# A first-pass timetable: the channel mix placed over all of its 4.5 slots, the input normalisation behind the key's high half

## The chip, the core and the metric

The kernel runs on one core of a Trainium2 chip. The metric is the device time of one execution, in microseconds (us). The core's engines are TensorE (PE, matmuls; PEld its weight loads), VectorE (DVE), ScalarE (ACT), GpSimd (POOL), and SyncE (SP), whose queue issues all of this kernel's DMAs. Each engine works through its own instructions in one order and stands where an instruction has to wait.

## The reference

The input `x` has 8 sequences of 1024 tokens and 512 channels. It is normalised, and two layers work on the result `xn`; their outputs are added to `x`.

```python
xn  = layernorm(x)
out = x + attn(xn) + ffn(xn)

# attn: Performer attention (16 heads of 32, 128 random features), then an MLP
pq, pk = phi(q), phi(k)         # exp(proj - |u|^2/2 - max(proj)) / sqrt(128) + 1e-6
kv, z  = sum_s pk v, sum_s pk   # over all 1024 tokens of a sequence
h      = (pq kv) / (pq z) @ wo
x1     = layernorm(xn + h) * g1 + b1
attn   = layernorm(x1 + gelu(x1 @ w1 + b1) @ w2 + b2) * g2 + b2

# ffn: channel mix with the token before
xr, xk = mu_r*xn + (1-mu_r)*xn_prev, mu_k*xn + (1-mu_k)*xn_prev
ffn    = sigmoid(xr @ Wr) * (relu(xk @ Wk)**2 @ Wv)
```

## The kernel before

Every large matmul is done in float16 with a high and a low half of each operand: `mm3` adds up high x high, high x low and low x high, 12 matmuls of 128x128 by 512 over four slices of 128 channels. So each operand is first made in float32, copied to float16 on ACT (the high half), and subtracted from its copy on DVE or POOL (the low half).

**Two passes.** In the first the tokens go in units of 128 (64 units, `i` or `b, u`) through normalisation, value, key, key features and the sums `kv` and `z`; beside it the channel mix layer (`ffn_k`, `ffn_r`, `ffn_o`) goes through blocks of 512 tokens (16 blocks, `bk`). The second pass does queries, attention output and the MLP. Between them the pools of the key are closed and those of the query opened.

**The timetable.** All work is written as generators that are entered with `at(tau, f, ...)`, where `tau` is a due time in slots of 15.4 us (`us(t)` is t / 15.4 slots). A heap takes the step that is due next and emits its instructions; `yield d` puts the rest of the generator back, due `d` later. So due times do not time anything on the chip: they fix the order of instructions on each engine. In the first pass the order on PE, DVE, ACT, POOL and SP is pinned to the order of emission (`Pinned`, `chained`). At slot 72.55 (`TK`) all but PE are let go of, until slot 81.55, and the scheduler of the framework orders them.

**A slot of the first pass**, with due times in us within the slot: the weights' product for the key (`proj_a`) on PE at 2.56, its high half `u` on ACT at 5.21, low half `u` on DVE at 6.41, its store `ud` and transposed copy `uT` on SP at 7.61, the three loads of `skk` (`proj_l`) on SP at 10.6; the key's norm (`norm`): POOL at 12.6, which reads `uT`, ACT 4.0 and DVE 10.0 later. The key features (`KB`), two parts a slot: PE at 9.0 and 14.56, then a maximum `mxk` and the bias `bik` on DVE, eight exps and a high half `ekh` on ACT, a low half `ekl` on DVE. The value (`V`): PE at 9.45, ACT at 12.15, DVE low half `v` at 13.65. `KC`, `KD`, `KE` add up and divide the sums (`kvp`, `kvz`, bank `kac`). Statistics of the input (`Ls`, `Lr`) are on DVE. `Ln` normalises a unit: ACT Identity in place on `xt`, ACT high half, POOL low half, then on SP a transposing DMA into `xb` and the store `xn_d`. One unit of `Ln` is due each slot, and `V` reads it three slots later.

**PSUM.** The results of `V` (`psv`), `proj_a` (`psu`), `ffn_k` (`psk`), `ffn_r` (`psr`) and `ffn_o` (`psf`) take turns in three banks (`mmt`), so a matmul group may start only when the result of three groups earlier has been read, by DVE's low half in the case of `V` and `proj_a`. `KB` has two buffers of its own, `pj`.

**The channel mix.** `ffn_k`, `ffn_r` and `ffn_o` have 12 groups a block, in spots at 0, 5.12 and 12 us of a slot, every ninth spot left out; a block thus takes 4.5 slots. `tau` of a block is the due time of its first `ffn_k`. What that reads is made by `mix(bk, p)`, called for p = 0 and 1, two channel slices (`w`) each: POOL adds the halves of `xb` to `xs` (513 columns) and takes the difference `df` of neighbouring tokens; DVE makes `xm` for k and for r from them; then for k and for r ACT writes the high half of `mx` and DVE the low half (1024 columns, two slices). `xs` and `df` have one buffer each, `xm` two. The first `ffn_k` takes the slices of p = 0 first and those of p = 1 behind them.

Of the kernel before, what the change touches and what calls it, by code (L numbers as in the profile page):

```python
# [11 lines left out]
F16 = mybir.dt.float16  # L12
# [11 lines left out]
BLK = 512  # L24
# [36 lines left out]
def block_kernel(ctx, tc, x, wq, wk, wv, wo, om3, ln1_g, ln1_b, w1, b1, w2, b2,  # L61
# [100 lines left out]
    def st(shape, dt, name, bufs=2, tag=None):  # L162
        tag = tag or name
        pool = pools["k"] if tag in KPOOL else pools["c"] if tag in CPOOL else pools["q"] if tag in QPOOL else sp
        return pool.tile(shape, dt, name=name, tag=tag, bufs=bufs)
# [25 lines left out]
    def us(t):  # L191
        return t / 15.4
# [14 lines left out]
    def warp(j, t):  # L207
        while t >= 27.68:
            j, t = j + 1, t - 27.68
        if j not in warps:  # L210
            r, tab = 0.0, []
            for a, d in slot_pe(j):
                d = max(d, 0.02)
                tab.append((a, r, d))
                r += d
            warps[j] = tab, r
        tab, ln = warps[j]
        a, r, d = [e for e in tab if e[0] <= t + 1e-6][-1]
        nx = min([e[0] for e in tab if e[0] > t + 1e-6], default=27.68)
        return TM + j + (r + (t - a) / (nx - a) * d) / ln  # L220
# [316 lines left out]
    mixd = {}  # L537
    kact = {}
    rr = {}

    def mix(bk, p):
        b, blk = divmod(bk, 2)
        hh, ll = xblk[b, blk]
        if p == 0:
            mixd[bk] = {nm: st([128, 2, 4, BLK], F16, "mx4", 4) for nm in "kr"}
        xm = {nm: st([128, 2, BLK], F32, "xm", 2) for nm in "kr"}
        o = XO - 1
        for w in range(2):
            c = p * 2 + w
            xs = st([128, BLK + 1], F32, "xs", 1)  # L550
            gps.tensor_tensor(xs, hh[:, c, o:o + BLK + 1], ll[:, c, o:o + BLK + 1], ALU.add)
            yield us(1.5)
            df = st([128, BLK], F32, "df", 1)
            gps.tensor_tensor(df, xs[:, 1:BLK + 1], xs[:, 0:BLK], ALU.subtract)
            yield us(4.0)
            for nm, mu in (("k", muk), ("r", mur)):
                dve.scalar_tensor_tensor(
                    xm[nm][:, w], df, mu[:, c:c + 1], xs[:, 0:BLK], ALU.mult, ALU.add
                )
                yield us(1.2)  # L560
        yield us(1.2)
        cs = slice(p * 2, p * 2 + 2)
        for nm in "kr":
            m = mixd[bk][nm]
            act.copy(m[:, 0, cs, :], xm[nm])
            yield us(3.2)
            dve.tensor_tensor(m[:, 1, cs, :], xm[nm], m[:, 0, cs, :], ALU.subtract)
            yield us(0.4)

    def ffn_k(bk, d):  # L570
        if d == 0:
# [282 lines left out]
    def at(tau, f, *a):  # L854
        ev.append((tau, len(ev), f, a))
# [17 lines left out]
    for i in range(NU):  # L873
        b, u = divmod(i, 8)
        at(i - 5 + us(0.5) if i > 5 else -9, Lx, i)
        at(i - 4 + us(4.9) if i > 3 else -7, Ls, i)
        if u % 4 == 0:
            at(i - 1 + us(7.3) if i else -6, Lr, i // 4)
        at(i + us(3.3) if i > 3 else -5 + 0.1 * i, Ln, b, u)
        if u % 4 == 3:  # L880
            at(i + 1.5, xstore, b, u // 4)
        at(i + 3 + us(9.45), V, b, u)
        at(i + 4 + us(2.56), proj_a, "k", b, u)
        at(i + 4 + us(10.6), proj_l, "k", b, u)
        at(i + 4 + us(12.6), norm, "k", b, u)
        at(i + 5 + us(9.0), KB, b, u, 0)
        at(i + 5 + us(14.56), KB, b, u, 1)
        at(i + 7 + us(7.7), KC, b, u)
        if u >= 4:
            at(i + 8 + us(2.53), KD, b, u - 4)  # L890
            at(i + 9 + us(7.65 if b < NB - 1 else 0.0), KE, b, u - 4)
# [4 lines left out]
    for bk in range(NBK):  # L896
        for k, (nm, a) in enumerate(GR):
            tau = spots[bk * 12 + k]
            if k == 0:
                for p in range(2):  # L900
                    at(tau - 2.7 + 1.25 * p, mix, bk, p)
            at(tau, {"k": ffn_k, "r": ffn_r, "o": ffn_o}[nm], bk, a)
    for k in range(32):
        at(12.3 + 1.5 * k, split_mlp, k)
# [4 lines left out]
    for i in range(NU):  # L909
        b, u = divmod(i, 8)  # L910
# [35 lines left out]
    for n in range(NBK):  # L946
        for t in range(4):
            if n == 0:
                tau = TQ + 6.5 + 0.3 * (t // 2) + 0.01 * (t % 2)
# [23 lines left out]
        for fc in range(16):  # L973
            s = j + fc // 4
            k = fc % 4
            tau = warp(s, (0.0, 2.56, 10.84, 16.56)[k])
# [34 lines left out]
    while todo:  # L1011
        tau, k, f, a = heapq.heappop(todo)
# [59 lines left out]
```

## Time and profile before

| | us |
|---|---|
| three runs, median (lowest to highest) | 3019.23 (3014.38 to 3019.41) |
| the profiled execution | 3021.76 |
| its span, first to last instruction | 3020.0 |
| TensorE busy in it | 2798.8 (93%) |
| VectorE, ScalarE, GpSimd busy | 2306.8, 1756.3, 990.9 |
| mean granted TensorE clock | 0.972 |

All times in the prediction's sums are from the one profiled execution. A busy time is the union of an engine's instructions in a stretch; an idle stretch is put down to what was released last before the instruction that ended it. A line such as `PE psk L137 <- DVE mx L185: 15.6, 6, 5.9` says that TensorE, ahead of matmuls that write `psk`, waited 15.6 us in total for a DVE instruction that writes `mx`, in 6 places, the longest 5.9. L137 and L185 are lines of helpers through which every instruction goes, so rows are told apart by tiles.

### The profile page before, as it was taken

What the parts mean: (1) busy time and instruction counts of PE and PEld (TensorE: products, weight loads), DVE (VectorE), ACT (ScalarE), POOL (GpSimd) and SP (SyncE); (2) the same over time, 40 slices, a digit from 0 to 9 for tenths busy, and PEclk for the clock granted to TensorE, in tenths of its full rate; (3) what the DMA queues carried; (4) which work ended last, traced back from release to release, by engine and by line L of the source; (5) the groups of instructions that cost most, each with busy time, mean ns of one, the idle gap of its engine ahead of it and who ended that gap; (6) DMA issues with size and microseconds to landing.
All of it is one profiled execution on the core that took longest, in us unless ns stands there. A gap on an engine that the chain in (4) does not pass through costs nothing. (4 is left out here: it accounts for less than half of the span.)

```text
span 3020.0 us, 52198 instructions
## 1 busy us (share of the span) xinstructions
PE 2798.8 (93%) x18784; PEld 1392.0 (46%) x18784; DVE 2306.8 (76%) x4456; ACT 1756.3 (58%) x3828; POOL 990.9 (33%) x860
## 2 busy tenths in 40 slices
PE   3999999999999884999999999999999999999996
PEld 1454444444445442444444444444444444444442
DVE  5898888888888756567777777777787787787654
ACT  4888888888888654454554554554554544554210
POOL 3444444554444323123222232232232232232111
PEclk7999999999999997999999999999999999999998
DMA  6567666666665288877777777777687677776432
GB/s 192 142 168 180 172 165 170 171 178 172 171 161 139 70 192 182 189 161 176 177 164 175 179 167 174 168 175 177 167 179 172 166 182 172 161 187 155 122 101 84
DMA packets 839348, 494.82 MB, mean 164 GB/s; under 512 B 632016, under 2 KB 718128, under 8 KB 837040
## 3 DMA queue, kind: packets, MB, share of 16 engines
q1 hardware_dynamic: 839088, 491.49, 66.6%
q8 instruction: 147, 2.41, 0.3%
q14 instruction: 113, 0.93, 0.1%
HBM read 226.95 MB, written 113.38 MB: 113 GB/s over the span
## 5 line engine op out<-in xcount | busy, mean ns | idle before, releaser
L137 PE MATMUL psw<-x1b,w1s 128*128 128x512 f16 x3072 | 695.3, 380 | 0.0
L137 PE MATMUL acc<-w2h,gg 128*128 128x512 f16 x2048 | 650.6, 380 | 2.0 <-DVE gg L185 1.9
L137 PEld LDWEIGHTS <-w1s 128*128 128x128 f16 x3072 | 295.9, 98 | 343.8 <-issue 2.5
L137 PEld LDWEIGHTS <-gg 128*128 128x128 f16 x3072 | 293.6, 98 | 329.0 <-issue 4.4
L185 ACT ACTIVATE g<-psw,b1t 128x512 f32<-128x512 f32 x256 | 172.7, 686 | 394.5 <-PE psw L137 351.4
L137 PE MATMUL acc<-w2l,gg 128*128 128x512 f16 x1024 | 389.1, 380 | 0.0
L185 ACT ACTIVATE e<-pj,biq 128x128 f32<-128x128 f32 x1024 | 291.9, 370 | 153.8 <-DVE biq L185 121.5
L185 ACT ACTIVATE e<-pj,bik 128x128 f32<-128x128 f32 x1024 | 280.9, 393 | 106.5 <-DVE bik L185 106.3
L185 POOL TENSOR_TENSOR eq<-e,eq 128x512 f16<-128x512 f32 x128 | 167.3, 1307 | 415.9 <-ACT eq L185 271.3
L185 POOL TENSOR_TENSOR u<-ot,u 128x512 f16<-128x512 f32 x64 | 84.1, 1314 | 662.4 <-ACT u L185 638.0
L185 DVE TENSOR_REDUCE mxq<-pj 128x4 f32<-128x512 f32 x256 | 175.2, 686 | 118.6 <-PE pj L137 117.6
L185 POOL TENSOR_TENSOR e<-u 128x512 f32<-128x512 f16 x128 | 174.3, 1361 | 181.0 <-DMA u<-u 160.6
L185 ACT ACTIVATE u<-psu 128x512 f16<-128x512 f32 x128 | 76.4, 597 | 235.9 <-PE psu L137 233.4
L185 DVE TENSOR_SCALAR gg<-g 128x512 f16<-128x512 f32 x256 | 107.9, 422 | 132.9 <-ACT g L185 132.8
L185 DVE SCALAR_TENSOR_TENSOR gg<-g,gg 128x512 f16<-128x512 f32 x256 | 188.9, 738 | 8.8
L137 PE MATMUL psv<-whv,xb 128*128 128x512 f16 x512 | 166.5, 387 | 20.0 <-DMA xb<-u 20.0
L137 PE MATMUL psu<-xb,whk 128*128 128x512 f16 x512 | 159.3, 394 | 27.6 <-DVE v L185 21.5
L185 ACT ACT_TABLE_LOAD x114 | 146.3, 1283 | 61.0 <-DVE biq L185 53.5
L185 DVE SCALAR_TENSOR_TENSOR ekl<-e,ekh 128x1024 f16<-128x1024 f32 x128 | 180.6, 1411 | 0.2
L137 PE MATMUL psk<-mx,whfk 128*128 128x512 f16 x512 | 157.2, 386 | 18.2 <-DVE mx L185 18.0
L137 PE MATMUL psf<-whfv,kx 128*128 128x512 f16 x512 | 163.4, 381 | 9.9 <-DVE u L185 9.9
L137 PE MATMUL psr<-whfr,mx 128*128 128x512 f16 x512 | 167.6, 390 | 2.2 <-DVE v L185 1.5
(160 smaller groups left out, 5627.1 us busy)
## 6 DMA issues: line engine op xcount, KB each, us to landing
w1s<-w1d SPq DMA_DIRECT2D x256, 256.0 KB, 3.0
ud<-u SPq DMA_DIRECT2D x128, 256.0 KB, 2.7
skk<-ud SPq DMA_DIRECT2D x192, 128.0 KB, 2.7
skq<-ud SPq DMA_DIRECT2D x192, 128.0 KB, 3.2
xt<-in_x SPq DMA_DIRECT2D x64, 256.0 KB, 3.5
xnd<-xt SPq DMA_DIRECT2D x64, 256.0 KB, 2.4
xtd<-xb SPq DMA_DIRECT2D x16, 1024.0 KB, 5.8
ffd<-rsg SPq DMA_DIRECT2D x64, 256.0 KB, 2.4
```

The lines of the kernel that those rows point to most:

```text
L137: return chained("pe", nc.tensor.matmul(*a, **k))
L185: return lambda *a, **k: chained(self.key, f(*a, **k))
```

## The change

The heap, the generators' instructions and their number stay; due times change, and with them the order on ACT, DVE, POOL and SP.

- `mix` gets a third argument `f`. From `df` to the first `xm` it waits 3.0 instead of 4.0 us, between the `xm` steps and behind them 2f instead of 1.2, from a high half to its low half 3.0 instead of 3.2, behind the low half 2f instead of 0.4. A pair of slices takes 15 + 14f us up to the due time of its last low half.
- The two halves of `mix` were due at tau − 2.7 and tau − 1.45 slots and overlapped. Now they follow one another: the first starts at tau − 4.5, but not before 4bk + 3.95 (when the block's last unit has been normalised); the second at tau − 2.3, or half-way from the first to tau − 0.3 where there is less room. `f` is worked out so that each fills its time. It is −0.11 in block 0, 0.07 in block 1, 0.44, 0.62, 0.99 in blocks 2 to 4, and 1.35 and 1.13 for the two halves from block 6 on.
- The buffers of `mx` are taken when the first high half is written, not at the start of `mix`.
- `Ln` is due at 5.6 instead of 3.3 us of its slot: its Identity and high half on ACT come behind the key's high half (5.21), and its two DMAs behind `ud` and `uT`.

```diff
-    def mix(bk, p):
+    def mix(bk, p, f):
         b, blk = divmod(bk, 2)
         hh, ll = xblk[b, blk]
-        if p == 0:
-            mixd[bk] = {nm: st([128, 2, 4, BLK], F16, "mx4", 4) for nm in "kr"}
+        mixd.setdefault(bk, {})
...
             gps.tensor_tensor(df, xs[:, 1:BLK + 1], xs[:, 0:BLK], ALU.subtract)
-            yield us(4.0)
+            yield us(3.0)
             for nm, mu in (("k", muk), ("r", mur)):
                 dve.scalar_tensor_tensor(
                     xm[nm][:, w], df, mu[:, c:c + 1], xs[:, 0:BLK], ALU.mult, ALU.add
                 )
-                yield us(1.2)
-        yield us(1.2)
+                yield us(2.0 * f)
+            yield us(2.0 * f)
         cs = slice(p * 2, p * 2 + 2)
         for nm in "kr":
+            if p == 0:
+                mixd[bk][nm] = st([128, 2, 4, BLK], F16, "mx4", 4)
             m = mixd[bk][nm]
             act.copy(m[:, 0, cs, :], xm[nm])
-            yield us(3.2)
+            yield us(3.0)
             dve.tensor_tensor(m[:, 1, cs, :], xm[nm], m[:, 0, cs, :], ALU.subtract)
-            yield us(0.4)
+            yield us(2.0 * f)
...
-        at(i + us(3.3) if i > 3 else -5 + 0.1 * i, Ln, b, u)
+        at(i + us(5.6) if i > 3 else -5 + 0.1 * i, Ln, b, u)
...
             if k == 0:
-                for p in range(2):
-                    at(tau - 2.7 + 1.25 * p, mix, bk, p)
+                m0 = max(4 * bk + 3.95, tau - 4.5)
+                m1 = max((m0 + tau - 0.3) / 2, tau - 2.3)
+                at(m0, mix, bk, 0, ((m1 - m0) * 15.4 - 15.0) / 14.0)
+                at(m1, mix, bk, 1, ((tau - 0.3 - m1) * 15.4 - 15.0) / 14.0)
```

## The prediction

> **What bounds the kernel now.** I read the page's engine shares and slices first, then busy time by stage, then TensorE's waits in the first pass, then VectorE's rows ahead of the longest wait. From the page:
>
> ```profile
> PE 2798.8 (93%) x18784; PEld 1392.0 (46%) x18784; DVE 2306.8 (76%) x4456; ACT 1756.3 (58%) x3828; POOL 990.9 (33%) x860
> ...
> PE   3999999999999884999999999999999999999996
> DVE  5898888888888756567777777777787787787654
> ACT  4888888888888654454554554554554544554210
> ```
>
> TensorE (PE) is the bound nearly everywhere; in the first third VectorE (DVE) and ScalarE (ACT) are nearly as full. By stage (start, first pass, changeover, second pass; columns: busy time and count per engine, then granted clock):
>
> ```profile
> 0.00:110.00 110.00, 61.27 (x343) 28.37 (x344) 68.78 (x132) 66.53 (x131) 43.50 (x49) 0.86 0.60 164
> 110.00:1010.00 900.00, 847.77 (x6252) 439.00 (x6251) 774.27 (x1253) 747.13 (x1717) 423.90 (x406) 0.98 0.64 167
> 1010.00:1240.00 230.00, 164.62 (x1215) 83.27 (x1214) 138.92 (x285) 121.95 (x297) 71.23 (x62) 0.84 0.70 160
> 1240.00:3020.00 1780.00, 1725.17 (x10980) 841.40 (x10977) 1324.87 (x2788) 820.66 (x1687) 452.26 (x344) 0.99 0.69 163
> ```
>
> The edited steps lie in the first pass and its two ends. There TensorE idles 900 − 847.8 = 52 us. The 472 high key matmuls (8 a slot) make 59 slots in those 900 us: 15.25 us each. Who TensorE waits for there (total, times, longest):
>
> ```profile
> PE psk L137 <- DVE mx L185: 15.6, 6, 5.9
> PE psu L137 <- DVE v L185: 12.4, 9, 2.5
> PE psf L137 <- DVE u L185: 9.9, 5, 3.1
> PE pj L137 <- ACT e L185: 7.7, 6, 2.3
> ...
> PE psr L137 <- DVE v L185: 1.5, 1, 1.5
> ```
>
> The first row is the mix itself: `ffn_k` stands until the second pair's low half of `mx` is written. Rows 2, 3 and 5 are PSUM banks that VectorE frees late (the low halves `v` and `u`). The longest wait on VectorE:
>
> ```profile
> 338.84 0.68 DVE L185 SCALAR_TENSOR_TENSOR rsg<-rsg,psf 128x512 f32<-128x512 f32 x1
> 339.44 1.22 DVE L185 TENSOR_REDUCE mxk<-pj 128x8 f32<-128x1024 f32 x1
> ...
> 343.05 1.22 DVE L185 TENSOR_TENSOR mx<-xm,mx 128x1024 f16<-128x1024 f32 x1
> 344.18 0.68 DVE L185 SCALAR_TENSOR_TENSOR v<-psv,v 128x512 f16<-128x512 f32 x1
> ```
>
> VectorE has no gap here; it works through a queue some microseconds behind the timetable, and `psk` starts as `mx` ends (344.3, after 5.94 idle).
>
> **The change, part by part.** No instruction is added or removed; every mix instruction, and the five of `Ln`, change place in an order fixed per engine.
>
> *1. The wait on `mx`.* Before, the second pair starts at tau − 1.45 slots and its k low half falls due 18.2 + 3.2 = 21.4 us later: 0.93 us ahead of `ffn_k`. After, for blocks 6 to 15, it starts at tau − 2.3 with f = 1.13, and is due 9 + 12f + 3 = 25.5 us later: 9.9 us ahead. (Block 0: 7.4, block 2: 8.5, block 4: 9.6.) The longest wait is 5.9, the move 6.5 to 9, so all go: 15.6, and 2.5 of the same kind at the start: **−18**.
>
> *2. The clock behind those waits.* Ten microseconds around the waits at 344 and at 894, and around one of 2.5 us at 202:
>
> ```profile
> 195.00:205.00 10.00, 7.47 (x43) 3.58 (x41) 9.83 (x17) 6.94 (x15) 1.76 (x4) 1.00 0.76 212
> 338.00:348.00 10.00, 4.06 (x12) 1.46 (x11) 9.83 (x17) 4.80 (x12) 1.22 (x2) 0.66 0.72 210
> ...
> 890.00:900.00 10.00, 6.85 (x27) 2.74 (x26) 9.53 (x13) 7.12 (x15) 4.20 (x5) 0.83 0.44 119
> ```
>
> 0.83 over 10 us is 1.7 us of lost clock. Seven 512-column matmuls at 634 instead of 379 ns after the wait make the same 1.8. Three of the `mx` waits (344, 757, 894) have such a stretch: **−5**. The Trainium skill, "TensorE: Matmul & The Clock Gate", section "Why this matters for your kernels", asks only that idle gaps stay under about 3 us; by it the 2.04 us gap at 757 would cost nothing, which the granted clock there (0.83) denies, and this term would be −3.4.
>
> *3. The banks.* Mix work on VectorE is, per block, 8 `xm` at 0.90 and 4 `mx` at 1.27 (means over all): 12.3 us. Before, it falls due between tau − 2.3 and tau + 0.2, 2.5 slots, 4.9 us a slot; after, over 3.9 slots, 3.1. VectorE is busy 774 / 59 = 13.1 a slot, so 13.1 − 12.3 / 4.5 = 10.4 without the mix: 15.3 in a mix slot before, as much as a slot lasts (15.25), and 13.5 after. The bank waits lie where that predicts: at 408, 470, 591, 683, 819, 836 and 954, each in the last two slots ahead of a block's tau. `Ln` behind the key's high half helps the same rows: its two ACT steps (0.83 and 0.62 us) no longer delay `u`, for which VectorE waits 69.3 us in 31 places. Rows: 12.4 + 9.9 + 2.2 = 24.5, and three slow-clock stretches (408, 470, 539), 5: between 0 and −30, and above nothing if VectorE comes to wait more (first rival). The mechanism fits but each wait has other feeders, so half: **−15**.
>
> *4. ACT.* `pj <- e`, 7.7 us with two stretches, 3.4: between 0 and −11. Its exps wait for `bik`, which VectorE computes late in the same slots; I take **−3**. `Ln`'s high half now stands between the exps of `KB`'s second part, ahead of all of which it stood before; no exp has more ahead of it.
>
> *5. What `Ln` passes.* On POOL its subtraction goes from 4.7 to 7.0 us, on SP the transposing DMA and the `xn_d` store from 7.3 to 9.6, behind `ud` and `uT` (7.61), ahead of the three `skk` loads (10.6). So the key's store no longer stands behind 1.24 us of transposing issue, 0.58 of store issue and the POOL step they wait for: its gain is at most the `pj <- skk` row, 3.1; I count none. `V` reads `xb` three slots later, so that reader is safe. The mix reads it at 4bk + 3.95 in blocks 0 to 5, 0.33 slot (5 us) after the due issue, and `xb` lands in 3.1 us (median); a late transfer stops POOL with the key norm behind it. POOL is 47% busy, so **0**; without that cover up to some 3 us in each of five blocks, +15.
>
> *6. Ends of the pass.* In the changeover TensorE waits 9.9 us for `kvz` while blocks 14 and 15 are mixed: between 0 and −10 (and their clock), I take **−3**. The order there is free of the timetable for a while and may shuffle by as much again; the second pass (waits of 31 us in 1780) keeps its steps.
>
> *7. What is late next.* −18 − 5 − 15 − 3 − 3 = −44 over 63 slots takes 0.7 us off a slot of 15.25. VectorE then fills 13.1 / 14.55 = 90% and ACT 747 / 59 / 14.55 = 87% (86% and 83% now), both in strict order: waits on banks and `pj` come back elsewhere. I give back a third, between nothing and all of parts 3 to 6 (21): **+15**.
>
> Sum **−29**. The profiled execution took 3021.8 (span 3020.0), 2.5 over the median, so 3021.8 − 29 − 2.5 = 2990.
>
> **The rivals.**
>
> *VectorE waits for POOL (slower).* Each pair of `xm` steps stands behind `df` on POOL. The lead from `df`'s due time to theirs shrinks from 4.0 to 3.0 us, while `xs` and `df` take 1.38 and 1.30; and in the later odd blocks the first `xs` now falls due 0.2 us behind the key norm's add, which waits for its transposed tile:
>
> ```profile
> POOL e L185 <- DMA u<-u: 92.2, 29, 7.9
> ...
> DVE xm L185 <- POOL df L185: 10.4, 7, 2.2
> ```
>
> Were half of the 64 pairs to wait 2.2 us, VectorE would lose 70 instead of 10. It decides against the change once more than the sure gain, 18 + 5 = 23 us, of new stall reaches TensorE; if half of the 60 does and the other parts give nothing, the sum is +7, if three quarters, +22: 3026 to 3041. For it: the seven such waits now. Against: the first `xs` and `df` of even blocks now stand ahead of the norm's add, and the norm comes earlier with the key; today's VectorE stalls (69 + 18 + 10) leave only 24.5 of bank waits.
>
> The Trainium skill, "SBUF — State Buffer", section "Who interferes with whom", speaks against spreading: a VectorE step with two SBUF inputs and a GpSimd step exclude each other. `xm` shows it (735 ns at best, 1698 at worst); if all 128 met one collision, it would be 128 × (1.70 − 0.90) = 102 us more of VectorE, and a mix slot as full as before.
>
> *Only the `mx` waits go.* VectorE's queue is late for other reasons, and half of 23 comes back at the banks: −12, 3007. For it: `psk` waits are the only ones that name the mix. Against: the places in part 3.
>
> *All waits of VectorE's queue go.* −18 − 5 − 30 − 11 with little given back: −50, 2969. For it: nothing but TensorE would then bound the pass. Against: 90% on two engines in strict order.
>
> *It doesn't spread.* Blocks 0 and 1 get less room than before (0.9 and 1.0 slot a pair; f is −0.11 and 0.07), and a POOL that runs late pushes the early steps back to where they were: within 6 us of 3019.
>
> **How the numbers follow.** Forecast (2975 to 3001) 0.45; only `mx` (3001 to 3013) 0.20; all waits (under 2975) 0.13; no spread 0.06; POOL stalls (over 3025) 0.16. 0.2%, about what a measurement of this kernel tells from no change, is 6 us: faster 0.78, same 0.06, slower 0.16. The range 2960 to 3030 cuts the tails of the third and the first rival.
>
> **What would show it.** Right: no `psk <- mx` row; the bank rows at half or less; first pass shorter by some 25 us at a clock of 0.99; the second pass at 1780. Wrong: `xm <- df` over 50 us with bank waits as before or more; POOL waiting for `xb`; or the time saved by 1010 lost again before 1240.

## The result, and the profile after

The changed kernel takes 3022.9 us (median of 17 runs, 3016.1 to 3025.2) against 3017.6 for the kernel before in the same session: a ratio of 1.0017, 95% interval [1.0009, 1.0024]. It is a little slower, by 5 us; 2990 was forecast, with 2960 to 3030 as the range and 0.78 on faster. The time lies in the range; the sign and nearly everything in the sum are wrong.

The profiled execution has a span of 3022.2 us. Its page and its busy times by stage (columns as before):

```profile
PE 2799.8 (93%) x18784; PEld 1392.2 (46%) x18784; DVE 2346.4 (78%) x4456; ACT 1752.7 (58%) x3828; POOL 990.1 (33%) x860
```

```profile
0.00:110.00 110.00, 64.40 (x345) 29.07 (x346) 69.44 (x130) 65.66 (x130) 43.98 (x49) 0.86 0.59 168
110.00:1010.00 900.00, 841.66 (x6195) 434.41 (x6193) 806.16 (x1249) 738.11 (x1704) 422.58 (x405) 0.98 0.63 164
1010.00:1240.00 230.00, 167.62 (x1262) 86.15 (x1259) 144.04 (x289) 126.28 (x308) 72.26 (x62) 0.84 0.70 164
1240.00:3020.00 1780.00, 1726.17 (x10992) 842.53 (x10990) 1326.77 (x2789) 822.67 (x1689) 451.26 (x344) 0.99 0.68 163
```

VectorE is where something new stands. Between 110 and 1010 it is busy 806 us with 1249 instructions, where it was 774 with 1253. The work is the same; its instructions have become longer. TensorE's waits in that stage:

```profile
PE psu L137 <- DVE v L185: 34.6, 18, 5.3
PE pj L137 <- ACT e L185: 7.8, 5, 1.9
PE psr L137 <- DVE v L185: 3.7, 4, 1.4
PE kac L137 <- DVE kvb L185: 3.0, 3, 1.3
PE psr L137 <- DVE u L185: 3.0, 3, 1.5
PE psf L137 <- DVE u L185: 2.5, 2, 1.3
```

The row `psk <- mx`, 15.6 us, is gone as forecast. In its place `psu <- v` went from 12.4 us in 9 places to 34.6 in 18: banks that VectorE's low half of the value frees late. The longest of these waits ends at 589.5. First VectorE ahead of it, then GpSimd in the same microseconds (start, duration):

```profile
584.49 1.04 DVE L185 TENSOR_TENSOR kvp<-kvp,kvr 128x132 f32<-128x132 f32 x1
585.57 1.16 DVE L185 CAST kvz<-kvp 128x132 f16<-128x132 f32 x1
586.76 1.05 DVE L185 TENSOR_TENSOR kvz<-kvp,kvz 128x132 f16<-128x132 f32 x1
587.73 1.11 DVE L185 SCALAR_TENSOR_TENSOR bik<-mxk,nsqk 128x8 f32<-128x8 f32 x1
588.76 0.68 DVE L185 SCALAR_TENSOR_TENSOR v<-psv,v 128x512 f16<-128x512 f32 x1
```

```profile
583.39 1.99 POOL L185 TENSOR_TENSOR u<-e,u 128x512 f16<-128x512 f32 x1 [3.71 <-ACT e L185]
585.34 1.20 POOL L185 TENSOR_TENSOR xs<-xb 128x513 f32<-128x513 f16 x1
...
586.62 1.04 POOL L185 TENSOR_TENSOR df<-xs 128x512 f32<-128x512 f32 x1
587.62 1.20 POOL L185 TENSOR_TENSOR e<-u 128x512 f32<-128x512 f16 x1
```

The first four VectorE steps are small: where nothing disturbs them they take 0.30, 0.23, 0.30 and 0.15 us, 1.0 together. Here they take 4.4. Each begins beside a GpSimd step and ends within 0.2 us after it. `v`, which reads PSUM, takes its usual 0.68. So 3.4 of TensorE's 5.34 us of waiting fall on four small steps that GpSimd held up one after the other. `xs` and `df` are the mix's (second pair of block 8): their new due places, 10.78 and 12.28 us of a slot, lie beside `KD` (11.13) and `bik` (11.3), and the key norm's sum (`e`) follows at 12.6. Blocks 6, 10, 12 and 14 have the same places.

**A measure for that.** For each form of VectorE instruction I took its tenth percentile as the undisturbed duration and added up what instructions took beyond it, where that was over 0.15 us ("held up" below). Between 110 and 1010 it is 92 us in 153 instructions before and 128 us in 197 after. 175 of the 197 end as if they had begun only when a GpSimd step ended (the two times agree within 0.15 us); the other 22 are `xm`, which end about 0.5 us after a GpSimd step. The step that ends so is the mix's `xs` or `df` for 21.5 us before and 37.9 after, and the low half of `Ln` (`u<-xt,u`) for 5.4 and 15.8. Most of the growth of 36 us lies in the small steps, here rows of before and then of after (mean ns behind the comma):

```profile
L185 DVE SCALAR_TENSOR_TENSOR bik<-mxk,nsqk 128x8 f32<-128x8 f32 x119 | 31.3, 263 | 1.8
...
L185 DVE TENSOR_TENSOR kvp<-kvp,kvr 128x132 f32<-128x132 f32 x28 | 12.5, 448 | 1.0
...
L185 DVE CAST kvz<-kvp 128x132 f16<-128x132 f32 x28 | 11.7, 416 | 1.0
```

```profile
L185 DVE SCALAR_TENSOR_TENSOR bik<-mxk,nsqk 128x8 f32<-128x8 f32 x118 | 41.9, 355 | 1.4
...
L185 DVE TENSOR_TENSOR kvp<-kvp,kvr 128x132 f32<-128x132 f32 x28 | 19.2, 685 | 1.0
L185 DVE CAST kvz<-kvp 128x132 f16<-128x132 f32 x28 | 17.0, 609 | 1.0
```

### The profile page after: what moved, and what is told of

Same layout as the page of the kernel before. It is cut to its first block, busy times and chain, and to the rows that moved or that the text cites. A ratio compares the mean times of both kernels' runs of the same rounds, so it can differ in the third digit from the quotient of the medians.

```text
span 3022.2 us, 52191 instructions
## 1 busy us (share of the span) xinstructions
PE 2799.8 (93%) x18784; PEld 1392.2 (46%) x18784; DVE 2346.4 (78%) x4456; ACT 1752.7 (58%) x3828; POOL 990.1 (33%) x860
## 5 line engine op out<-in xcount | busy, mean ns | idle before, releaser
L185 ACT ACTIVATE e<-pj,bik 128x128 f32<-128x128 f32 x1024 | 288.1, 387 | 132.8 <-DVE bik L185 132.6
L137 PE MATMUL psu<-xb,whk 128*128 128x512 f16 x512 | 165.8, 408 | 48.7 <-DVE v L185 41.5
L185 POOL TENSOR_TENSOR e<-u 128x512 f32<-128x512 f16 x128 | 166.4, 1300 | 131.2 <-DMA u<-u 113.2
L185 ACT CAST eq<-e 128x512 f16<-128x512 f32 x256 | 158.3, 621 | 11.7 <-DMA pq<-eq 4.4
```

Source lines behind the costliest of these rows:

```text
L137: return chained("pe", nc.tensor.matmul(*a, **k))
L185: return lambda *a, **k: chained(self.key, f(*a, **k))
```

## The experiments

The table compares all runs. "Ratio" is to the kernel before, with its 95% interval; "pass" is the time from the key's product (`psu`) of unit 5 to that of unit 63 in the profiled execution (the expectations call them slots 5 and 63; in the timetable they are due in slots 9 and 67); the last three columns are VectorE's busy time between 110 and 1010, what it waited there (the sum of its rows of waits), and what it was held up. All but the ratio come from one profile per kernel. The executions of the kernel before differ by up to 7 us, so 2 or 3 us in a pass are no finding by themselves. "Held up" repeats better: e10 to e12, which leave GpSimd's work as it was, have 91 to 92, as before.

| run | ratio | pass | busy | waits | held up |
|---|---|---|---|---|---|
| before | 1 | 882.0 | 774 | 111 | 92 |
| after | 1.0017 [1.0009, 1.0024] | 890.3 | 806 | 79 | 128 |
| e1, mix alone | 1.0053 [1.0040, 1.0066] | 897.2 | 789 | 98 | 115 |
| e2, `Ln` alone | 1.0004 [0.9995, 1.0013] | 878.3 | 791 | 95 | 105 |
| e3, mix half a slot ahead | 1.0045 [1.0033, 1.0058] | 896.4 | 776 | 110 | 106 |
| e4, the same with `Ln` | 1.0028 [1.0017, 1.0039] | 887.3 | 797 | 89 | 118 |
| e5, before, less GpSimd | 0.9840 [0.9826, 0.9853] | 839.9 | 743 | 143 | 33 |
| e6, e3, less GpSimd | 0.9844 [0.9830, 0.9857] | 847.8 | 745 | 139 | 42 |
| e7, after, less GpSimd | 0.9815 [0.9801, 0.9828] | 838.2 | 764 | 119 | 54 |
| e8, `Ln` from unit 8 on | 0.9981 [0.9972, 0.9990] | 876.8 | 789 | 96 | 105 |
| e9, before, GpSimd fills | 0.9922 [0.9909, 0.9934] | 846.5 | 749 | 137 | 49 |
| e10, more VectorE | 1.0069 [1.0056, 1.0082] | 902.6 | 795 | 89 | 92 |
| e11, less VectorE | 0.9948 [0.9936, 0.9961] | 867.8 | 757 | 128 | 92 |
| e12, no wait for `mx` | 0.9988 [0.9979, 0.9997] | 880.4 | 775 | 110 | 91 |

**The two parts of the change, each by itself.** e1 has the new `mix` and the old `Ln`, e2 the reverse:

```diff
-        at(i + us(5.6) if i > 3 else -5 + 0.1 * i, Ln, b, u)
+        at(i + us(3.3) if i > 3 else -5 + 0.1 * i, Ln, b, u)
```

Expected of e1:

> The spread of the mix alone, with the normalisation at 3.3 us as before. Theory 1 (the spread puts GpSimd steps beside VectorE steps that cannot run with them: VectorE was busy 774 us between 110 and 1010 before and 806 after, at the same number of instructions): VectorE is busy 795 us or more there, the bank waits psu <- v are 25 us or more, and the time is 3 to 10 us over before. Theory 2 (the moved normalisation is what stretches VectorE, since its GpSimd step now meets the small steps at 10 to 11.3 us): VectorE busy stays within 8 us of 774, the psk waits are gone, and the time is 8 to 20 us under before.

Expected of e2:

> The normalisation at 5.6 us alone, the mix as before. Theory 1: VectorE busy stays within 8 us of 774, its wait u <- u falls from 69 to about 20 us, and the time is 2 to 10 us under before. Theory 2: VectorE is busy 795 us or more, and the time is 3 to 10 us over before.

The spread alone costs 16 us of time and 15 of the pass. Of theory 1 the bank waits came out (28.0), not VectorE's busy time (789, not 795) nor the size of the loss (3 to 10); theory 2 has the sign wrong. VectorE is held up 22 us more; it also waits 33.7 us for `df` (10.4 before, 15.5 in the changed kernel): the prediction's first rival is real here. How much of the 15 us is its doing was not separated.

```profile
PE psu L137 <- DVE v L185: 28.0, 15, 4.8
```

```profile
DVE xm L185 <- POOL df L185: 33.7, 20, 4.8
DVE u L185 <- ACT u L185: 33.5, 15, 4.3
```

`Ln` alone shortens the pass by 3.7; on top of the spread (after against e1) it gives 6.9. Its mechanism shows in VectorE's row `u <- ACT u`, here before and then in e2:

```profile
DVE u L185 <- ACT u L185: 69.3, 31, 5.0
```

```profile
DVE u L185 <- ACT u L185: 43.8, 20, 4.2
```

Its time is the same as before; the start is 5 us longer (unit 5's key product begins at 119.4 instead of 114.3). So neither theory's time came out, and the row fell to 43.8, not to about 20. VectorE's busy time is 791, 13 of the 16 more being held up. So the move of `Ln` stretches VectorE too, nearly as theory 2 has it, but it takes away more waits than it adds.

**The wait removed without a spread.** e3 keeps the old spacing of `mix` and moves it ahead; e4 adds the new `Ln` (with 3.95 in place of 3.65):

```diff
+                d = min(0.5, max(0.0, tau - 2.7 - (4 * bk + 3.65)))
                 for p in range(2):
-                    at(tau - 2.7 + 1.25 * p, mix, bk, p)
+                    at(tau - 2.7 - d + 1.25 * p, mix, bk, p)
```

Expected of e3:

> The old spacing of the mix, moved half a slot (7.7 us) ahead from block 2 on, the normalisation as before: so the mx waits go without a spread. Theory 1: VectorE busy within 10 us of 774, psk waits under 3 us, time 5 to 20 us under before. Theory 3 (VectorE's queue as a whole sets the pass, and a wait that is taken from psk comes back at the banks wherever the mix stands): the psk waits go, psu <- v rises by about as much (to 25 us or more), and the time is within 5 us of before.

Expected of e4:

> The same half slot, with the normalisation at 5.6 us. Theory 1: the sum of the two runs before it, 8 to 30 us under before, VectorE busy under 785. Theory 2: as slow as the normalisation alone, VectorE busy 795 or more. Theory 3: within 5 us of before, with bank waits in place of psk.

No theory expected e3's time. Theory 3 had the waits right (`psu <- v` at 25 us or more), and a time within 5 us of before wrong. The `psk <- mx` row went, VectorE's order differs only in where the mix steps stand, and the pass is 14 us longer. TensorE's waits came back, with more, at the banks (12.4 before) and at the exps (7.7 before):

```profile
PE psu L137 <- DVE v L185: 25.2, 16, 4.1
PE pj L137 <- ACT e L185: 16.5, 11, 2.7
```

VectorE is held up 14 us more. e4 is 9 us shorter in the pass than e3, `Ln`'s gain once more; its VectorE time (797) is theory 2's, its time, 9 us over before, nobody's. Taking the waits for `mx` away had bought nothing, which left two questions: what the holding up costs, and what those waits were worth.

**Less to be held up by.** e5 is the kernel before with three GpSimd steps left out, e6 and e7 are e3 and the changed kernel with the same edit:

```diff
-        gps.tensor_tensor(uu.rearrange("p t h k -> p t (h k)"), uT[:, 0], uT[:, 1], ALU.add)
+        u0 = uT[:, 0].rearrange("p t (h k) -> p (t h) k", h=4)
...
-        act.activation(uu, uu, AF.Square, scale=1.0 / SU)
+        act.activation(uu, u0, AF.Square, scale=1.0 / SU)
...
-            df = st([128, BLK], F32, "df", 1)
-            gps.tensor_tensor(df, xs[:, 1:BLK + 1], xs[:, 0:BLK], ALU.subtract)
+            df = xs[:, 1:BLK + 1]
...
-        gps.tensor_tensor(k4[:, 1, d, :], kr, k4[:, 0, d, :], ALU.subtract)
```

Expected of e5:

> The order of before, with three GpSimd steps left out: the key's and query's norm squares the high half alone, the mix uses the sum one token on in place of the difference, and the low half of the squared relu is not made (its matmul takes the high half again). 219 of GpSimd's 424 us between 110 and 1010 go, nothing is added elsewhere. Theory 1 (VectorE steps that GpSimd holds up cost the pass as much as they are stretched): VectorE busy falls by 40 to 55 us to about 725, the time by 20 to 50. Rival (order: what counts is which VectorE step stands ahead of the ones that free banks): VectorE busy falls as much, the time by under 10.

Expected of e6:

> The mix half a slot ahead, with the same three GpSimd steps left out. Whole, the shift was 14 us slower than before, and VectorE busy was larger by the same 14 us in the pass. Theory 1: with GpSimd's steps gone the shift is within 5 us of the run before it, or faster. Rival (order): still 10 us or more slower than the run before it.

Expected of e7:

> The changed kernel with the same three GpSimd steps left out. Theory 1: 8 to 25 us faster than the order of before without these steps, psu <- v under 15 us. Rival (order): no faster than it, psu <- v 25 us or more.

No engine but GpSimd has less to do, and 48 us of time go, 42 of them in the pass, as theory 1 expected; VectorE is held up 33 us in place of 92.

```profile
110.00:1010.00 900.00, 866.98 (x6477) 451.47 (x6476) 742.87 (x1302) 770.09 (x1768) 211.33 (x248) 0.99 0.65 167
```

More instructions fit into the 900 us, so VectorE is busy 743 us there, not the 725 expected. With these GpSimd steps gone the whole times go theory 1's way: the shift is level with the order of before (+1.8 us), and the changed order is faster by 7.6 us (2960.8 to 2963.1 against 2967.8 to 2971.1), just under what was expected. Its `psu <- v` is 11.3 us. The pass says less: the shift's is still 8 us longer than e5's, the changed order's only 1.7 shorter, and the rest of the 7.6 lies in the changeover (171.9 us against 178.2). VectorE is still held up 42 and 54 us in them, against 33. So these two runs don't show that the new order of the mix would pay in the pass without GpSimd.

e9 asks whether GpSimd's time did it, or its reading. Each of the three steps is replaced by two fills of the same tile, for instance

```diff
-            gps.tensor_tensor(df, xs[:, 1:BLK + 1], xs[:, 0:BLK], ALU.subtract)
+            for _ in range(2):
+                gps.memset(df, 0.0)
```

Expected:

> The order of before; the same three GpSimd steps each replaced by two fills of the tile that they wrote, which read nothing and hand the tile on as the step did (so the key's and query's norm squares the high half alone, the mix adds no difference, and the low half of the squared relu is zero). Theory 1 (what costs is that VectorE and GpSimd cannot both read): VectorE busy between 110 and 1010 stays at 735 to 755 as without the steps, and the time within 10 us of 2969. Rival (it was GpSimd's time and queue, not the exclusion): VectorE busy back to 765 or more and the time to 3000 or more.

```profile
110.00:1010.00 900.00, 861.13 (x6458) 448.38 (x6456) 749.32 (x1295) 768.37 (x1767) 375.78 (x589) 0.99 0.64 167
```

GpSimd is busy 376 us there instead of 211 in e5, nearly the 424 of before, and the pass is 846.5: within 7 us of e5, 36 short of before. So it was not GpSimd's time but its reading. The single steps show it too: of the `bik` that began while a fill had over 0.15 us left, 0 of 30 were held up, beside a GpSimd step that reads 9 of 10 in the same run (24 of 33 before). The same holds for `ekl`, `xm` and the subtraction for `kvz`, all with two inputs in SBUF. Fills did hold up two kinds of step with a single input, the cast to `kvz` (17 of 22) and `nsqk` (13 of 20), by 0.2 us each. (The fills also wait for no inputs; but VectorE's own waits for `df`, 2.6 us here and 10.4 before, are too small to be the 36.) The whole time, 2995, misses the 10 us that theory 1 expected (VectorE's 749 meets it); the second pass of this run is some 20 us longer than in the others; its `pj <- e` waits are as many as in e5 (14) and longer (33.7 against 25.8 us), which I did not follow up. That lies behind the first pass and doesn't touch its reading.

**What VectorE's time is worth.** e10 makes the statistics of each unit from 12 on twice, e11 leaves out the low half of the r mix:

```diff
+        if i >= 12:
+            stats(pools["k"], xts[i], xmv[n][:, k, :], "L")
```

```diff
-            dve.tensor_tensor(m[:, 1, cs, :], xm[nm], m[:, 0, cs, :], ALU.subtract)
+            if nm == "k":
+                dve.tensor_tensor(m[:, 1, cs, :], xm[nm], m[:, 0, cs, :], ALU.subtract)
...
-        mm3(ps, (m[:, 0], m[:, 1]), W["fr"], lambda a, c: a[:, c, tt], lambda a, c: a[:, c, :])
+        mm3(ps, (m[:, 0], m[:, 0]), W["fr"], lambda a, c: a[:, c, tt], lambda a, c: a[:, c, :])
```

Expected of e10:

> The order of before, with the statistics of each unit from 12 on (one bn_stats of 0.69 us on one input and one small aggregate of 0.18 us) made twice in the same place: 52 units by 0.8 us, 42 us more of VectorE in the first pass. Theory 4 (VectorE's own queue, busy plus its stops, sets the length of the pass, though it is busy only 86%): the time rises by 25 to 45 us. Rival (its 14% of idle time takes them in): under 10 us.

Expected of e11:

> The order of before, with the low half of the r mix left out on VectorE (its matmul takes the high half again): 32 steps of 1.27 us, 41 us, two in each block; the k mix and its waits are untouched. Theory 4: the time falls by 25 to 40 us. Rival (TensorE bounds the pass and VectorE matters only by the psk waits): under 10 us.

Both land between the two theories: 42 us more of VectorE give +21 us of time (+20.6 in the pass), 41 us less −16 (−14.2). An idle share of 14% takes in half to two thirds; a microsecond of VectorE's work in the first pass is worth 0.35 to 0.5. The runs with less GpSimd give more for each microsecond that VectorE is held up less: 42 us of pass for 59 in e5, 36 for 43 in e9, 49 for 64 from e3 to e6, 52 for 74 from after to e7, so 0.7 to 0.8. These edits also take waits for GpSimd's results away, from VectorE and ScalarE; how much of the difference that is was not separated.

**What the wait for `mx` was worth.** e12 leaves every engine but TensorE as it was and takes away TensorE's reason to wait:

```diff
-        mm3(ps, W["fk"], (m[:, 0], m[:, 1]), lambda t, c: t[:, c, ds], lambda t, c: t[:, c, :])
+        mm3(ps, W["fk"], (m[:, 0], m[:, 1]), lambda t, c: t[:, c, ds], lambda t, c: t[:, c % 2, :])
```

> The order of before on every engine; the first product of the channel mix reads the first pair's two slices of the k mix twice, in place of the second pair's, so TensorE has nothing to wait for at the mix, while VectorE, ScalarE and GpSimd do exactly what they did. Prediction's steps 1 and 2 (each of these waits is worth its length and the slow clock behind it): the psk waits go, and the first pass between slots 5 and 63 is 15 to 21 us shorter than 882, the time 14 to 25 under before. Theory 4 (VectorE is the queue that sets the pass, and it runs without a gap through these waits): the psk waits go, others rise by at least half of them, and the pass is less than 7 us shorter.

```profile
PE psf L137 <- DVE u L185: 20.3, 7, 3.9
PE psu L137 <- DVE v L185: 13.6, 12, 2.7
```

The pass is 1.6 us shorter, the whole time 3.6 (0.9 to 6.3 by its interval), as theory 4 expected. Of 15.6 us of waiting, `psf <- u` alone took back 10.4, `psu <- v` 1.2 and `psk` at its bank 4.2. VectorE did the same work at the same pace (775 busy, 91 held up), and TensorE, arriving earlier, waited for the next thing VectorE owed it.

**A version that is faster.** e8 has the mix of before and the new `Ln` from unit 8 on, so that the start is as it was:

```diff
-        at(i + us(3.3) if i > 3 else -5 + 0.1 * i, Ln, b, u)
+        at(i + us(3.3 if i < 8 else 5.6) if i > 3 else -5 + 0.1 * i, Ln, b, u)
```

> The mix as before; the normalisation at 5.6 us from unit 8 on, units 4 to 7 at 3.3 as before. With all units from 4 on at 5.6 the pass was 4 us shorter from slot 5 to 63 and the start 5 us longer. If both are as read, this one keeps the 4 and loses the 5: start within 1 us of before, time 3 to 8 us under before. If the start's 5 us is a chance of the order that comes back elsewhere: within 3 us of before.

3012.4 us against 3017.5: 5 us under before, ratio 0.9981 [0.9972, 0.9990], and under the changed kernel too. The pass is 5 us shorter. The start kept 2 of its 5 us (unit 5 at 116.2), so the start within 1 us of before did not come out.

## Why the prediction was wrong, point by point

**Step 1, −18: failed, and it is the largest term.** The waits went as worked out. But the sum took them as time saved. The rows shown for it say otherwise: VectorE had no gap through the longest of them. The trace has more: in all 25 waits of TensorE for VectorE in the stage before, 40.4 us, VectorE has no gap of over 0.1 us. A wait in which the engine waited for works without pause is that engine's backlog seen from TensorE; e12 gives for the 15.6 us 1.6 of the pass and 3.6 of the time. Step 2 (−5 for the clock behind these waits) falls with it: other waits took their place, and the clock of the stage is 0.98 as before, with eight stretches at half clock instead of nine.

**Step 3, −15: failed, and took the other sign.** Bank waits rose from 24.5 us (12.4 + 9.9 + 2.2) to 43.8 (34.6 + 3.7 + 3.0 + 2.5). The load per slot was worked out from means, as if the spread changed no duration. In the 2.5 slots from 2.3 ahead of a block's first product (blocks 2 to 12) VectorE was busy 14.2 us a slot before, not 15.3, and 14.0 after, not 13.5; in the slots between these stretches it went from 11.7 to 13.3. So the full slots hardly emptied, and the others filled. Nor do all the waits listed lie ahead of a block: after the one at 836 the next block begins at 889. I priced the exclusion of VectorE and GpSimd for the mix's own `xm` steps, which hardly changed (held up 18.1 us before, 17.5 after), and not for the small steps beside which the GpSimd steps of the mix and of `Ln` came to stand: `bik`, `nsqk`, `kvp` and `kvz` were held up 42 us before and 71 after, 30 of the 36 more. Alone, the spread adds 22 us of holding up (e1) and `Ln` 13 (e2). The Trainium skill, "SBUF — State Buffer", section "Who interferes with whom", had the rule, and the runs agree with it: the second of the two waits until the first is done; steps that read PSUM (`v`, `u`) and `tensor_reduce` (`mxk`, mean 1214 ns before, 1213 after) are not held up; fills of GpSimd, which read nothing, hold up no step with two SBUF inputs and little in all (e9). It was weighed as an argument against the change and then given no term in the sum.

The part of step 3 that rests on `Ln` was right: `u <- u` fell from 69.3 to 43.8 us by itself (e2) and to 17.9 with the spread, and the move is worth 4 to 9 us of the pass in three pairs of runs (e2 to before, after to e1, e4 to e3), its own holding up included.

**Step 4, −3:** 7.7 us before, 7.8 after; nothing. **Step 5, 0:** right on the transfers (GpSimd waited 0.3 us for `xb`), but the moved subtraction of `Ln` on GpSimd holds VectorE up 10 us more, which had no term. **Step 6, −3:** `kac <- kvz` rose to 11.6. The changeover as a whole went the other way: from the first of the query's products (`psu`) to the eleventh it takes 173.5 us instead of 181.5, mostly because TensorE waits 19.8 us for `pq` instead of 30.8. It lies between 172 and 179 in all other runs, whatever was changed, so the profiled execution of before had a long one; why is open. It hides most of the pass's loss: −0.6 at the start, +8.3 in the pass, +2.9 to the first query product, −8.0, −0.4 make the +2.2 of the two profiled spans. Part of the 8 may be that one execution's own: it took 4.2 us over the median of its kernel, the profiled one of after 1.1. **Step 7, +15:** right that time is given back, but waits come back because VectorE's queue is behind, not because TensorE gains on it, and far more than a third of it.

**The sum redone.** The spread alone is +15 in the pass: 22 us more held up at 0.35 to 0.5 make 8 to 11 and leave 4 to 7; at the 0.7 to 0.8 of the runs with less GpSimd they make 16 to 18, all of it. In e3, where 14 us more are held up, the two prices make 5 to 7 and 10 to 11 of the 14. So the holding up is between a third and all of the loss in these two runs; how large the rest is, from the longer waits for `df` or from mix steps that stand ahead of those that free banks, was not separated. `Ln` gives 7 back: +8.

**Rivals.** "Only the `mx` waits go", with its half given back, was nearest in kind and still too generous: in e12 more than half came back, by the pass nine tenths. The first rival (+7 to +22) had the sign and, with e1, part of the mechanism; in the changed kernel `xm <- df` is 15.5 us where it needed over 50.

## What to carry to other kernels

Before a wait is counted as a gain, look at the engine that is waited for: if it runs without a gap up to the release, the wait is its backlog and will come back at the next thing it owes; what counts is work or stops taken off that engine, here 0.35 to 0.5 us for a microsecond of work and 0.7 to 0.8 for one of holding up, with what else the GpSimd steps cost. When steps are moved on GpSimd, list the VectorE steps that they come to stand beside: here a step of 0.15 us with two SBUF inputs could take as long as a whole GpSimd step when it met one that reads. An order that is spread evenly is not better by that; which steps meet matters too.

## What was not expected of the hardware

A GpSimd step of 1.0 to 1.2 us made VectorE steps of 0.15 to 0.30 us last 1.04 to 1.16, four in a row. Nearly the same GpSimd time spent in fills (two of 0.53 us for each step) left the pass within 7 us of having no such steps at all, where the steps themselves cost 42.
